# A Mamba layer and a ternary FFN on one core: the FFN's second product from float32 to three bfloat16 passes, by halves of the tokens

## The chip, the core and the metric

The kernel runs on one core of a Trainium2 chip. Five engines work from queues of their own, each strictly in order: PE (TensorE, matrix products into PSUM), DVE (VectorE), ACT (ScalarE, with function tables that are loaded when the function changes), POOL (GpSimd) and SP, which here only issues DMAs. They meet through semaphores. The metric is the device time of one run in microseconds. Inputs lie in HBM; the work sits in SBUF (128 partitions) and in the eight banks of PSUM, 512 float32 wide each.

## The reference

16 sequences of 512 tokens, 256 wide, go through a Mamba-2 block and then an FFN with ternary weights, each with layer norms and residuals. The FFN is what the change touches:

```python
def _ternary(w):
    scale = jnp.maximum(jnp.mean(jnp.abs(w)), 1e-08)
    w_t = jnp.clip(jnp.round(w / scale), -1.0, 1.0)
    return w + jax.lax.stop_gradient(w_t - w)
...
    h = jnp.einsum('bsd,fd->bsf', x, _ternary(W1)) + b1      # 256 -> 1024
    h = jax.nn.gelu(h, approximate=False)
    out = jnp.einsum('bsf,df->bsd', h, _ternary(W2)) + b2    # 1024 -> 256
...
x = x + _layernorm(mamba branch of _layernorm(x))
x = x + _layernorm(_L0_ffn_ref(_layernorm(x)))
```

The ternary weights are -1, 0 and 1, so they are exact in bfloat16. A float32 number is, to float32 accuracy, the sum of three bfloat16 pieces: its head, the head of what is left, and what is left after that. A product of float32 activations with ternary weights is then three bfloat16 products that add up in one PSUM bank.

## The kernel before

Each sequence b goes through stages, written as Python generators that yield now and then an amount of work:

- `stage_a0`, `stage_t0`: first layer norm (x1) and its transpose x1T (tile pt_a).
- `stage_a`: input projection on PE, blocks pm (lines 320 to 340, with a convolution by DVE into cv and a SiLU by ACT into xbc) and pz (line 345, SiLU into zs), the rows of dt (pq, pqt). Block 5 of pm is `stage_a5`.
- `stage_a2`: softplus of dt in small DVE steps (lines 447 to 465, tiles sp_z, sp_e, sp_a), then sums (pd), whose exponentials are `stage_b0` (dec, cum; lines 507 and 512).
- `stage_b1`: the decay matrices mt by PE (pe, line 549) and ACT's Exp. `stage_d`, `stage_e`: ct by a DMA and three POOL products (line 533).
- `stage_b2`: the scan over four chunks of 128 tokens: PE's px, pg, pst and py, DVE's xdt, bT, mt, state and y, POOL's xend, zs, state and the squares (lines 573, 574).
- `stage_c1`: output projection po, second residual x2, the FFN's norm x3, its transpose pt_f, and the three bfloat16 pieces of the transposed x3 in the tile x3p: head by ACT (739), rest by DVE (740), head of the rest by ACT (743), third piece by POOL (744).
- `stage_c2`: the FFN. For each of 8 blocks f of 128 hidden channels, `passes` makes 6 matmuls of 512 columns (3 pieces, 2 halves of the 256 inputs) into a PSUM tile ph of its own, and ACT's GELU with its bias writes hT in float32 (762). Then, for each chunk c of 128 tokens, 8 float32 matmuls (790) with hT as the loaded and `w2_sb` as the moving side give pf; DVE adds b2 (796), and the last norm and the residual follow (`finish`, by DVE 290, POOL 782 and a DMA by SP).

`interleave` merges generators: each stream has a total work and a start and end between 0 and 1, and the next step is taken from the stream that is least far along. The queues are recorded in just that order, and all four compute engines run it as recorded. A turn i of the main loop (lines 885 to 909, i from 1 to 14) has two parts. In the first, `stage_a` of sequence i+1 runs beside `stage_c1` of i-1 and `stage_e` of i. In the second, `stage_c2` of i-1 runs beside `stage_b2` of i, with `a2`, `a5`, `b0`, `b1` and `a0` of later sequences at given places. After the loop come one interleaving for the last two sequences (lines 911 to 918) and `stage_c2(15)` by itself.

PSUM: four banks (`ps_a`) serve the projections and the scan, two (`ps_tr`) transposes and small results, two (`ps_c`) po, ph and pf. Before the loop `scales` and `ternary` make the ternary weights: `w1_bf` in bfloat16, w2 in place in float32.

## Time and profile before

| | |
|---|---|
| three timed runs | 1174.28, 1177.25, 1177.72 us; median 1177.25 |
| the profiled execution | 1172.91 us |
| its span, first to last instruction | 1171.1 us |
| mean granted clock of PE | 0.98 |
| first product, L756, PE | 768 records of 128x512 bf16, 189.0 us busy |
| second product, L790, PE | 1024 records of 128x256 f32, 248.8 us busy |
| GELU, L762, ACT | 128 of 128x512, 87.8 us busy, 688 ns each, and 15 table loads of 1283 ns |

Busy time is how long an engine had an instruction running; a matmul of N columns has a record longer than the time after which the next may start, so means of PE records overlap and the steady distance between starts is read from the chain of waits. A float32 matmul shows as two records. The idle time in front of an instruction is put down to what released it. In the windows each engine's busy time is given for a stretch, with the number of instructions in brackets. The trace's clock runs from the first instruction.

### The profile page before, as it was taken

The numbers are of one execution on the slowest core, as the hardware profiler recorded it, in microseconds if no ns is written. First come the engines' busy times: TensorE is split into PE (matmuls) and PEld (weight loads), VectorE is DVE, ScalarE is ACT, GpSimd is POOL, SyncE is SP. The second block draws the span as 40 slices with busy tenths as digits, with TensorE's granted clock in tenths as the row PEclk, the third lists the DMA queues.
The fourth block names the chain that finished last, engine by engine and source line by source line (L and its number), as shares of the span: only waits on it lengthen the run. The fifth ranks groups of instructions, "written<-read, shape, count | busy, mean of one in ns | idle before, by whom it ended". The sixth has DMA issues, their size and how long they took to land.

```text
span 1171.1 us, 16958 instructions
## 1 busy us (share of the span) xinstructions
PE 1110.8 (95%) x6164; PEld 727.9 (62%) x6164; DVE 849.0 (72%) x2211; ACT 568.0 (48%) x957; POOL 593.7 (51%) x706
## 2 busy tenths in 40 slices
PE   5778999999999999999999999999999999998697
PEld 2345475665757666575766757576675757667475
DVE  5597968768686876868687686868768686875552
ACT  5625546356454635645463564546346454532321
POOL 3453546355554635555463555546355554545742
PEclk9888999999999999999999999999999999999899
DMA  5101010020201102020110202011020101002000
GB/s 194 58 1 58 18 67 27 4 76 17 75 18 65 29 4 76 17 74 19 59 35 4 73 20 75 18 58 36 4 72 20 75 18 58 19 4 72 2 10 27
DMA packets 28627, 48.57 MB, mean 41 GB/s; under 512 B 6656, under 2 KB 25728, under 8 KB 26496
## 3 DMA queue, kind: packets, MB, share of 16 engines
q1 hardware_dynamic: 26992, 47.33, 11.8%
q8 instruction: 48, 0.79, 0.3%
q10 hardware_dynamic: 1552, 0.16, 0.1%
q14 instruction: 35, 0.29, 0.1%
HBM read 38.44 MB, written 9.04 MB: 41 GB/s over the span
## 4 chain that ended last, share of the span: by engine, by line
PE 83%; DVE 6%; POOL 6%; ACT 3%; DMA 1%; issue 1%; POOLq 0%; ACTq 0%; DVEq 0%
PE pf L790 20%; PE pm L323 12%; PE ph L756 12%; PE po L710 9%; PE pz L345 8%; PE py L644 5%; PE pst L628 4%; PE py L651 3%; POOL x3p L744 3%; PE pe L549 2%; DVE cv L330 1%; POOL xend L608 1%; PE pt_a L300 1%; PE px L593 1%; PE pt_f L736 1%
## 5 line engine op out<-in xcount | busy, mean ns | idle before, releaser
L790 PE MATMUL pf<-w_sb,hT 128*128 128x256 f32 x1024 | 248.8, 383 | 0.0
L330 DVE SCALAR_TENSOR_TENSOR cv<-pm,cw_sb,cv 128x511 f32<-128x511 f32 (+2 forms) x288 | 215.3, 747 | 44.8 <-ACT cv L328 36.9
L790 PEld LDWEIGHTS pf<-w_sb,hT 128*128 128x128 f32 x1024 | 189.8, 190 | 42.3 <-issue 14.3
L756 PE MATMUL ph<-x3p,w_bf 128*128 128x512 bf16 x768 | 189.0, 381 | 4.2 <-ACT x3p L743 1.7
L661 POOL TENSOR_TENSOR zs<-y,zs 128x512 f32<-128x512 f32 x64 | 81.7, 1276 | 206.9 <-DVE y L657 206.9
L323 PE MATMUL pm<-x1T,win_sb 128*128 128x512 f32 x384 | 184.1, 602 | 0.0
L762 ACT ACTIVATE hT<-ph,b_sb 128x512 f32<-128x512 f32 x128 | 87.8, 688 | 128.2 <-PE ph L756 128.2
L756 PEld LDWEIGHTS <-w_bf 128*128 128x128 bf16 x768 | 72.9, 98 | 93.8 <-issue 29.1
L553 ACT ACTIVATE mt<-pe 128x512 f32<-128x512 f32 x128 | 73.6, 595 | 110.3 <-PE pe L549 110.3
L710 PE MATMUL po<-wo_sb,zs 128*128 128x256 f32 x512 | 124.6, 388 | 0.3 <-DVE att L716 0.3
L345 PE MATMUL pz<-x1T,win_sb 128*128 128x512 f32 x256 | 123.8, 607 | 0.3 <-DVE dt L368 0.3
L328 ACT ACTIVATE cv<-pm,cw_sb 128x512 f32<-128x512 f32 x96 | 65.7, 684 | 118.7 <-PE pm L323 117.1
L323 PEld LDWEIGHTS pm<-x1T,win_sb 128*128 128x128 f32 x384 | 70.9, 193 | 71.8 <-issue 65.7
L710 PEld LDWEIGHTS po<-wo_sb,zs 128*128 128x128 f32 x512 | 95.8, 192 | 28.3 <-issue 16.9
L533 POOL TENSOR_TENSOR ct<-ct,xbc 128x1024 f32<-128x1024 f32 x48 | 113.3, 2374 | 0.0
L657 DVE SCALAR_TENSOR_TENSOR y<-xbc,dsk,py 128x128 f32<-128x128 f32 x256 | 71.2, 340 | 37.5 <-PE py L651 20.7
L644 PE MATMUL py<-mt,xdt 128*64 128x128 f32 x1024 | 97.0, 284 | 0.0
L796 DVE TENSOR_TENSOR o<-pf,b_sb 128x256 f32<-128x256 f32 x64 | 26.8, 419 | 88.2 <-PE pf L790 88.2
L349 ACT ACTIVATE zs<-pz 128x512 f32<-128x512 f32 x64 | 37.9, 592 | 93.3 <-PE pz L345 93.3
L345 PEld LDWEIGHTS pz<-x1T,win_sb 128*128 128x128 f32 x256 | 48.0, 194 | 55.9 <-issue 47.0
L611 DVE SCALAR_TENSOR_TENSOR mt<-mt,pg 128x1024 f32<-128x1024 f32 x64 | 77.6, 1212 | 0.5
L644 PEld LDWEIGHTS py<-mt,xdt 128*64 128x64 f32 x1024 | 61.3, 140 | 26.8 <-issue 11.8
(138 smaller groups left out, 1810.1 us busy)
## 6 DMA issues: line engine op xcount, KB each, us to landing
ct<-way SPq DMA_DIRECT2D x16, 1536.0 KB
xin<-in_x SPq DMA_DIRECT2D x16, 512.0 KB, 6.7
out<-o SPq DMA_DIRECT2D x30, 256.0 KB, 2.2
w_in<-in_w SPq DMA_DIRECT2D x1, 1024.0 KB
w_sb<-in_w SPq DMA_DIRECT2D x1, 1024.0 KB
win_sb<-in_w_in SPq DMA_DIRECT2D x1, 768.0 KB, 6.2
win_sb<-in_w_in SPq DMA_DIRECT2D x1, 512.0 KB
wo_sb<-in_w_out SPq DMA_DIRECT2D x1, 512.0 KB
```

The lines of the kernel that those rows point to most:

```text
L323: nc.tensor.matmul(pm, win_sb[:, k, DI + m * P : DI + (m + 1) * P], x1T[:, k, :], start=(k == 0), stop=(k == 1),)
L330: nc.vector.scalar_tensor_tensor(cv[:, j:], pm[:, 0 : L - j], cw_sb[:, m, 3 - j : 4 - j], cv[:, j:], ALU.mult, ALU.add,)
L345: nc.tensor.matmul(pz, win_sb[:, k, j * P : (j + 1) * P], x1T[:, k, :], start=(k == 0), stop=(k == 1),)
L533: nc.gpsimd.tensor_tensor(ct[:, c - 1], ct[:, c - 1], xbc[:, 5, c * P : (c + 1) * P].unsqueeze(1).to_broadcast([P, NH, P]), ALU.mult,)
L553: nc.scalar.activation(mt[:, hs, :].rearrange("p h t -> p (h t)"), pe, AF.Exp)
L611: nc.vector.scalar_tensor_tensor(mts[c], mts[c], 1.0, cbt.unsqueeze(1).to_broadcast([P, NH, P]), ALU.min, ALU.mult)
L644: nc.tensor.matmul(py[h % 2 * HD : (h % 2 + 1) * HD, j, :], xdt[:, h * HD : (h + 1) * HD], mts[c][:, h, :], start=True, stop=(c == 0),)
L661: nc.gpsimd.tensor_tensor(zs[:, :, tok], y, zs[:, :, tok], ALU.mult)
L710: nc.tensor.matmul(po[:, 0:DM], g[:, k, c * P : (c + 1) * P], wo_sb[:, k, :], start=(k == 0), stop=(k == NJ - 1),)
L756: nc.tensor.matmul(ph, w1_bf[:, k, f * P : (f + 1) * P], x3p[:, j, k, :], start=(j == 0 and k == 0), stop=(j == 2 and k == 1),)
L762: nc.scalar.activation(hT[:, f, :], ph, AF.Gelu, bias=b1_sb[:, f : f + 1])
L790: nc.tensor.matmul(pf[:, 0:DM], hT[:, f, c * P : (c + 1) * P], w2_sb[:, f, :], start=(f == 0), stop=(f == NF - 1),)
```

## The change

Three things change.

The first product's and the GELU's results are read as bfloat16 without a cast: `upper` views a float32 tile as pairs of bfloat16 and takes every second one, the upper half of the bits. For x3 the head is the upper half of a float32 copy (`x3h`), the rest is taken against it, and the rest's upper half is the second piece; only the third is a bfloat16 tile of its own (`x3t`). ACT's casts of line 743 are gone.

The FFN runs by halves of the tokens: 256 columns in each matmul of the first product, GELU into `h` (float32). Two blocks f and f+1 share one PSUM tile from block 2 on (in the second half from block 0 on); in the instruction order as built, the matmuls of the odd block wait for the GELU of the even one. For each pair of blocks DVE subtracts (`rest`, h minus its upper half, into `hr`) and POOL subtracts (`third`, into `ht`), at the places that `later` and the second loop give. The second product is three bfloat16 passes per half, each over both chunks and 8 blocks, into two PSUM tiles that stay open through all three.

The order moves: `stage_c2`'s work is given as 20.7 instead of 24.2 (so `b0`, at half of the part, now stands between the two halves of the tokens), `b1` comes later, and after the loop `stage_c1(14)` comes first, `stage_e(15)` earlier and `stage_c2(14)` from 0.235 on. SBUF tiles change their places accordingly (rests, the staging of w1 and w2).

```diff
@@ -180,13 +181,13 @@
     wo_sb = const.tile([P, DI // P, DM], F32)
     nc.sync.dma_start(wo_sb, w_out.rearrange("(k p) n -> p k n", p=P))
 
-    w1_in = one.tile([P, NF, L], F32, tag="hT", name="w1_in")
-    w1_sb = w1_in[:, 0 : 2 * FF // L, :].rearrange("p f t -> p (f t)").rearrange(
-        "p (k n) -> p k n", k=2
-    )
+    w1_in = one.tile([P, NF, L // 2], F32, tag="h", name="w1_in")
+    w1_sb = w1_in.rearrange("p f t -> p (f t)").rearrange("p (k n) -> p k n", k=2)
     nc.sync.dma_start(w1_sb, w1.rearrange("(k p) n -> p k n", p=P))
     w1_bf = const.tile([P, 2, FF], BF16)
-    w2_sb = const.tile([P, NF, DM], F32)
+    w2_in = one.tile([P, NF, L // 2], F32, tag="hr", name="w2_in")
+    w2_sb = w2_in.rearrange("p f t -> p (f t)").rearrange("p (k n) -> p k n", k=NF)
+    w2_bf = const.tile([P, NF, DM], BF16)
     nc.sync.dma_start(w2_sb, w2.rearrange("(k p) n -> p k n", p=P))
 
     negA = const.tile([P, NH], F32)
@@ -195,10 +196,11 @@
 
 
 
-    x3p_0 = one.tile([P, 3, 2, L], BF16, tag="x3p", name="low_2")
+    low_1 = one.tile([P, NF, L // 2], BF16, tag="ht", name="low_1")
+    low_2 = one.tile([P, 2, L], F32, tag="x3h", name="low_2").bitcast(BF16)
     ternaries = {
-        1: (w1_sb, w1_in[:, 4:8, :].rearrange("p f t -> p (f t)"), w1_bf),
-        2: (w2_sb, x3p_0.rearrange("p j k t -> p (j k t)")[:, 0 : 4 * L], w2_sb),
+        1: (w1_sb, low_1.rearrange("p f t -> p (f t)"), w1_bf),
+        2: (w2_sb, low_2.rearrange("p k t -> p (k t)"), w2_bf),
     }
     halves = {}
 
@@ -235,6 +237,10 @@
             )
             yield 1.0
 
+
+    def upper(t):
+
+        return t.bitcast(BF16).rearrange("p a (t i) -> p a t i", i=2)[:, :, :, 1]
 
     class Norm:
 
@@ -682,8 +688,6 @@
         last = b == NB - 1
         if last:
             x2 = io.tile([P, NC, DM], F32, tag="xin", name=f"x2_{b}")
-            rests = io.tile([P, NC, DM], F32, tag="xin", name=f"rests_{b}")
-            rests = rests.rearrange("p c d -> p (c d)").rearrange("p (k t) -> p k t", k=2)
         else:
             x2 = one.tile([P, NC, DM], F32, tag="x2", name=f"x2_{b}")
         x3 = one.tile([P, NC, DM], F32, tag="att", name=f"x3_{b}")
@@ -727,53 +731,32 @@
             yield (0.1, 0.07, 0.01, 0.33)[c]
         norm_f.normal(x3, 0, 1, 2, 3)
         yield 0.22
-        if not last:
-            rests = one.tile([P, 2, L], F32, tag="o", name=f"rests_{b}")
-        x3p = one.tile([P, 3, 2, L], BF16, tag="x3p", name=f"x3p_{b}")
+
+
+        if b < NB - 2:
+            rests = one.tile([P, NC, DM], F32, tag="att", name=f"rests_{b}")
+        else:
+            rests = three.tile([P, NC, DM], F32, tag="x1", name=f"rests_{b}")
+        rests = rests.rearrange("p c d -> p (c d)").rearrange("p (k t) -> p k t", k=2)
+        x3h = one.tile([P, 2, L], F32, tag="x3h", name=f"x3h_{b}")
+        x3t = one.tile([P, 2, L], BF16, tag="x3t", name=f"x3t_{b}")
         for k in range(2):
             pt = ps_tr.tile([P, 512], F32, tag="tr", name=f"pt_f{b}_{k}")
             for c in range(NC):
                 nc.tensor.transpose(
                     pt[:, c * P : (c + 1) * P], x3[:, c, k * P : (k + 1) * P], ident
                 )
-            nc.scalar.copy(x3p[:, 0, k, :], pt)
-            nc.vector.tensor_sub(rests[:, k, :], pt, x3p[:, 0, k, :])
+            nc.scalar.copy(x3h[:, k, :], pt)
+            nc.vector.tensor_sub(rests[:, k, :], pt, upper(x3h)[:, k, :])
         yield 0.12
         for k in range(2):
-            nc.scalar.copy(x3p[:, 1, k, :], rests[:, k, :])
-            nc.gpsimd.tensor_sub(x3p[:, 2, k, :], rests[:, k, :], x3p[:, 1, k, :])
-        s.update(x2=x2, x3p=x3p, shift=norm_c.off)
+            nc.gpsimd.tensor_sub(x3t[:, k, :], rests[:, k, :], upper(rests)[:, k, :])
+        s.update(x2=x2, x3=(upper(x3h), upper(rests), x3t), shift=norm_c.off)
 
 
     def stage_c2(b):
         s = seqs.pop(b)
-        x2, x3p, shift = s["x2"], s["x3p"], s["shift"]
-        hT = one.tile([P, NF, L], F32, tag="hT", name=f"hT_{b}")
-
-        def passes(ph, f, lo, hi):
-            for j in range(lo, hi):
-                for k in range(2):
-                    nc.tensor.matmul(
-                        ph, w1_bf[:, k, f * P : (f + 1) * P], x3p[:, j, k, :],
-                        start=(j == 0 and k == 0), stop=(j == 2 and k == 1),
-                    )
-
-        def bent(ph, f):
-            nc.scalar.activation(hT[:, f, :], ph, AF.Gelu, bias=b1_sb[:, f : f + 1])
-
-        phs = [ps_c.tile([P, L], F32, tag="c", name=f"ph_{b}_{f}") for f in range(2)]
-        for f in range(2):
-            passes(phs[f], f, 0, 2)
-            yield 0.86
-        for f in range(2):
-            passes(phs[f], f, 2, 3)
-            bent(phs[f], f)
-            yield 0.44
-        for f in range(2, NF):
-            ph = ps_c.tile([P, L], F32, tag="c", name=f"ph_{b}_{f}")
-            passes(ph, f, 0, 3)
-            bent(ph, f)
-            yield 1.3
+        x2, x3, shift = s["x2"], s["x3"], s["shift"]
         o = one.tile([P, NC, DM], F32, tag="o", name=f"o_{b}")
         norm_o = Norm(o, f"o{b}")
 
@@ -784,27 +767,83 @@
                 out[b].rearrange("(c p) d -> p c d", p=P)[:, lo:hi], o[:, lo:hi]
             )
 
-        for c in range(NC):
-            pf = ps_c.tile([P, L], F32, tag="c", name=f"pf_{b}_{c}")
-            for f in range(NF):
-                nc.tensor.matmul(
-                    pf[:, 0:DM], hT[:, f, c * P : (c + 1) * P], w2_sb[:, f, :],
-                    start=(f == 0), stop=(f == NF - 1),
-                )
-                if f % 2 == 1 and f < NF - 1:
-                    yield 0.86
-            nc.vector.tensor_tensor(o[:, c, :], pf[:, 0:DM], b2_sb, ALU.add)
-            norm_o.stats(c)
-            if b == NB - 1:
-                norm_o.shift(c, c + 1, shift)
-                finish(c, c + 1)
-                yield 0.86
-                continue
-            if c % 2 == 1:
-                norm_o.shift(c - 1, c + 1, shift)
-            if c == 2:
-                finish(0, 2)
-            yield 0.86
+        for half in range(2):
+            T = L // 2
+            tok = slice(half * T, (half + 1) * T)
+
+            h = one.tile([P, NF, T], F32, tag="h", name=f"h_{b}_{half}")
+            hr = one.tile([P, NF, T], F32, tag="hr", name=f"hr_{b}_{half}")
+            ht = one.tile([P, NF, T], BF16, tag="ht", name=f"ht_{b}_{half}")
+            pieces = upper(h), upper(hr), ht
+
+            def passes(ph, f, lo, hi):
+                for j in range(lo, hi):
+                    for k in range(2):
+                        nc.tensor.matmul(
+                            ph, w1_bf[:, k, f * P : (f + 1) * P], x3[j][:, k, tok],
+                            start=(j == 0 and k == 0), stop=(j == 2 and k == 1),
+                        )
+
+            def bent(ph, f):
+                nc.scalar.activation(h[:, f, :], ph, AF.Gelu, bias=b1_sb[:, f : f + 1])
+
+            def rest(p):
+                fs = slice(2 * p, 2 * p + 2)
+                nc.vector.tensor_sub(hr[:, fs, :], h[:, fs, :], pieces[0][:, fs, :])
+
+            def third(p):
+                fs = slice(2 * p, 2 * p + 2)
+                nc.gpsimd.tensor_sub(ht[:, fs, :], hr[:, fs, :], pieces[1][:, fs, :])
+
+            later = {3: (rest, 0), 5: (rest, 1), 6: (third, 0), 7: (rest, 2)}
+            first = 0
+            if half == 0:
+                phs = [ps_c.tile([P, L], F32, tag="c", name=f"ph_{b}_{f}") for f in range(2)]
+                for f in range(2):
+                    passes(phs[f][:, 0:T], f, 0, 2)
+                    yield 0.43
+                for f in range(2):
+                    passes(phs[f][:, 0:T], f, 2, 3)
+                    bent(phs[f][:, 0:T], f)
+                    yield 0.22
+                first = 2
+            for f in range(first, NF):
+                if f % 2 == 0:
+                    ph = ps_c.tile([P, 2, T], F32, tag="c", name=f"ph_{b}_{half}_{f}")
+                passes(ph[:, f % 2, :], f, 0, 3)
+                bent(ph[:, f % 2, :], f)
+                yield 0.65
+                if f in later:
+                    act, p = later[f]
+                    act(p)
+                if half == 1 and f == 4:
+                    finish(0, 2)
+
+            pfs = [ps_c.tile([P, L], F32, tag="c", name=f"pf_{b}_{half}_{c}") for c in range(2)]
+            for j in range(3):
+                for c in range(2):
+                    for f in range(NF):
+                        nc.tensor.matmul(
+                            pfs[c][:, 0:DM], pieces[j][:, f, c * P : (c + 1) * P], w2_bf[:, f, :],
+                            start=(j == 0 and f == 0), stop=(j == 2 and f == NF - 1),
+                        )
+                        if f % 4 == 3:
+                            yield 0.43
+                            if j == 0:
+                                for at, act, p in (
+                                    (3, third, 1), (7, rest, 3), (11, third, 2), (15, third, 3)
+                                ):
+                                    if at == 8 * c + f:
+                                        act(p)
+                    if j == 2:
+                        at = 2 * half + c
+                        nc.vector.tensor_tensor(o[:, at, :], pfs[c][:, 0:DM], b2_sb, ALU.add)
+                        norm_o.stats(at)
+                        if b == NB - 1 and half == 1:
+                            norm_o.shift(at, at + 1, shift)
+                            finish(at, at + 1)
+            if b < NB - 1 or half == 0:
+                norm_o.shift(2 * half, 2 * half + 2, shift)
         if b < NB - 1:
             endings.append(lambda: finish(2, 4))
 
@@ -835,7 +874,7 @@
     endings = []
     E_WORK = 1.0
     A0_WORK, T0_WORK, A_WORK, A2_WORK, B1_WORK, B2_WORK = 1.0, 0.9, 18.1, 1.0, 0.5, 14.9
-    C1_WORK, C2_WORK = 1.0, 24.2
+    C1_WORK, C2_WORK = 1.0, 20.7
 
 
 
@@ -894,8 +933,8 @@
             run(stage_a1(i + 1))
             second = [
                 (stage_b0(i + 1), 0.1, 0.5, 0.51),
-                (stage_b1(i + 1, 0, 2), 2 * B1_WORK, 0.68, 0.8),
-                (stage_b1(i + 1, 2, 3), B1_WORK, 0.86, 0.9),
+                (stage_b1(i + 1, 0, 2), 2 * B1_WORK, 0.77, 0.86),
+                (stage_b1(i + 1, 2, 3), B1_WORK, 0.88, 0.92),
                 (stage_b1(i + 1, 3, 4), B1_WORK, 0.95, 0.99),
             ]
             second.append((stage_c2(i - 1), C2_WORK, 0.02, 1.0))
@@ -909,12 +948,12 @@
             interleave(*second)
         run(stage_a6(NB - 1))
         interleave(
-            (ending(), 0.1, 0.05, 0.06),
-            (stage_e(NB - 1), E_WORK, 0.0, 0.25),
-            (stage_c1(NB - 2), C1_WORK, 0.0, 0.4),
-            (stage_b2(NB - 1), B2_WORK, 0.0, 0.53),
-            (stage_c2(NB - 2), C2_WORK, 0.4, 0.98),
-            (stage_c1(NB - 1), C1_WORK, 0.54, 1.0),
+            (ending(), 0.1, 0.0, 0.01),
+            (stage_c1(NB - 2), C1_WORK, 0.0, 0.235),
+            (stage_e(NB - 1), E_WORK, 0.03, 0.16),
+            (stage_b2(NB - 1), B2_WORK, -0.02, 0.4),
+            (stage_c2(NB - 2), C2_WORK, 0.235, 0.98),
+            (stage_c1(NB - 1), C1_WORK, 0.42, 0.9),
         )
         interleave((ending(), 0.1, 0.05, 0.06), (stage_c2(NB - 1), C2_WORK, 0.0, 1.0))
 
```

## The prediction

> **What bounds the kernel now.** First the table of busy times and the costliest groups, to see the engine that never rests and what the edited lines cost. Second the windows of one turn of the main loop. Third the chain of waits and the timeline, for how a wait of PE on ACT and a clash of DVE and POOL look.
>
> ```profile
> PE 1110.8 (95%) x6164; PEld 727.9 (62%) x6164; DVE 849.0 (72%) x2211; ACT 568.0 (48%) x957; POOL 593.7 (51%) x706
> L790 PE MATMUL pf<-w_sb,hT 128*128 128x256 f32 x1024 | 248.8, 383 | 0.0
> L756 PE MATMUL ph<-x3p,w_bf 128*128 128x512 bf16 x768 | 189.0, 381 | 4.2 <-ACT x3p L743 1.7
> ```
> ```profile
> 523.00:548.00 25.00, 24.46 (x107) 14.29 (x106) 23.10 (x56) 15.36 (x27) 16.23 (x18) 1.00 0.09 32
> 548.00:591.50 43.50, 43.50 (x281) 30.55 (x280) 28.88 (x83) 19.59 (x34) 19.45 (x26) 1.00 0.13 45
> ```
> The columns are length, PE, weight loads, DVE, ACT, POOL, clock. A turn lasts 68.5 us. Its second part, where the FFN of one sequence runs beside the state work of the next, has PE busy for all of 43.5 us, with DVE at 28.9 and POOL at 19.5: PE sets the turn, and the other two stay ahead of it because their queues have gaps.
>
> ```profile
> 485.77 0.44 PE px L593 x4
> 486.54 1.29 PE ph L756 x6
> ```
> ```profile
> 1142.26 0.70 ACT hT L762
> 1142.95 0.04 issue
> 1143.00 7.93 PE ph L756 x36
> ```
> The first pair prices PE: 0.215 us for a bfloat16 matmul of 512 columns, 0.109 for one pass of 128 columns in float32. The second, from the last sequence, is the one place where PE waits for a GELU: the next block can't start until ACT is through.
>
> ```profile
> 74.49 4.46 DVE L459 SCALAR_TENSOR_TENSOR sp_a<-sp_a,sp_e 128x32 f32<-128x32 f32 x4
> 80.50 2.27 DVE L463 SCALAR_TENSOR_TENSOR dt<-sp_a,dt 128x32 f32<-128x32 f32 x1
> ```
> ```profile
> 75.88 2.34 POOL L533 TENSOR_TENSOR ct<-ct,xbc 128x1024 f32<-128x1024 f32 x1
> 78.18 0.72 POOL L573 TENSOR_TENSOR y<-y 128x256 f32<-128x256 f32 x1
> 78.98 0.45 POOL L574 TENSOR_TENSOR sq<-y 128x128 f32<-128x128 f32 x1
> 79.39 1.04 POOL L633 TENSOR_TENSOR state<-state,dec 128x512 f32<-128x512 f32 x1
> 80.39 2.34 POOL L533 TENSOR_TENSOR ct<-ct,xbc 128x1024 f32<-128x1024 f32 x1
> ```
> A DVE operation with both inputs in SBUF, 0.19 us by its median, lasts as long as the POOL operation that is running, and the two engines take turns. The new DVE subtractions have both inputs in SBUF.
>
> **What PE saves.** Per sequence the second product is 32 float32 matmuls of 256 columns, two records each, at 1.73 us for 8 records: 13.8 us. It becomes 96 bfloat16 matmuls of 256 columns. No row has that shape. Lower bound: half of 0.215, 0.1075; upper bound: the load (98 ns mean on L756) not hidden, 0.205. I take 0.109, since the transposes on L593 hide a load of 143 ns under a pass of that length: 10.46 us. The first product goes from 48 matmuls at 0.215 (10.34) to 96 at 0.109 (10.46). Saved: 3.2 us a sequence, 51 over 16.
>
> Two of three pieces are read at every second bfloat16; no row shows such a read. Bounds: nothing, or 0.215 a matmul (the float32 records, 0.215 for 256 columns) for the 64 of 96 first-product matmuls whose moving side is spread, 64 x 0.106 = +6.8 us a sequence. I take nothing, the nearest row: the float32 transposes also step by four bytes and pass 128 columns in 0.109. The Trainium skill, "SBUF — State Buffer", section "Door 1: The DMA port swizzle", has 16-byte lines that give full bandwidth while at least two accesses fall in a line, which four-byte steps meet; by it the sum has no such term either, and a rate of half would refute it here.
>
> **What it adds.** *A wait at each odd block.* Two 256-column blocks of the first product now share a PSUM tile, and in the built order the odd block's first matmul waits for the GELU of the even one. Last matmul of the even block: its record of about 0.27 us (376 ns less the 107 of the missing columns) runs 0.16 past its stream; 0.03 to ACT; GELU of 256 columns 0.47 (0.69 for 512, less 256 x 0.84 ns, the slope between the copies of 128 and 512 columns, 265 and 587 ns); 0.04 back: 0.70 us. In one turn block 3 of the first half hides it under a pst (0.86), block 5 under a py (1.02), block 3 of the second half under a pm. Uncovered: block 7, and blocks 5 and 7 of the second half, 2.1 us. Block 1 of the second half is worse: `b0`'s exponentials now fall between the halves, so ACT loads tables twice more (1.28 each). From pd on: sums, copy of cum, load, dec, cum, load, GELU: about 0.9 us of stall. Against that, PE needs 3.6 us from pd to there.
>
> *DVE and POOL.* Per sequence 8 subtractions of 512 on DVE, 0.68 each (L740), 5.4 us; 8 on POOL at 1.16 (L744), 9.3 us, minus nothing, since the two for x3 stay. ACT loses the two casts on L743 (1.23), so x3's third piece starts some 2.2 us sooner; but block 2 waits for block 0's GELU behind the table load that ended at 547.13, PE idles 1.7 us there instead of 1.1: +0.6. DVE's 28.9 and POOL's 19.5 of the second part become 34.3 and 28.8 of 40.3. That fits as a share; it does not fit as a queue. I walked the built queues from 543.16 with the rows' durations:
> - First half, second pieces. PE: from block 2's start at 547.7 six blocks of 0.65, pst 0.86, py 1.02, the wait 0.70, px and pg 0.77, 20 matmuls of pf 2.2, pst 0.86, py 1.72: it asks for blocks 4 to 7 at 559.7. DVE's queue up to rest 3, from the first y at 551.7: y 1.1, four softplus steps 0.8, rest 1 0.68, xdt 0.69, pg and bT 0.6, mt 1.2, four softplus steps 0.8, rest 2 0.68, state 0.69, rest 3 0.68. POOL's: zs up to 554.1, third 0 555.3, xend 556.3, third 1 557.5, the squares 558.7, state 559.7. With no clash DVE's state waits for that, and rest 3 ends at 561.1: a stall of 1.2. With clashes the softplus steps wait out zs and third 0, the next four get one turn per POOL operation (third 1, two squares, state), so rest 2 ends at 563.1, and rest 3, behind third 2, at 565.0: 5.1.
> - pd then waits for the softplus, queued behind rest 3: 0.1 or 1.3.
> - `b1`'s fourth exponent needs the PSUM bank that the last y frees; y stands behind rest 1 and the output's scaling: 1.2 or 1.55. The second half's second pieces then: 0 or 2.1.
> - Third pieces of the second half. When the last py ends POOL still has rs and off (1.2), the output's addition (1.27), third 0, the squares, zs behind that y, and thirds 1 to 3: by the walk 10.6 us without clashes, 12.9 with. PE asks after 6.7 or 8.5 and gets 4 matmuls in between: 3.4 or 3.9.
>
> Sum without clashes 0.6+2.1+0.9+1.2+0.1+1.2+0+3.4 = 9.5, with them 0.6+2.1+0.9+5.1+1.3+1.55+2.1+3.9 = 17.55. Less 3.2: +6.3 or +14.3 us a turn. I take two thirds of the way up, +11.7, since the clashes are shown but not each falls in step.
>
> *Clock.* After PE's idle 3.9 us up to 1090.75 and 3.2 up to 1096.87, the four pairs of py took 0.43 instead of 0.22 us, until 1106. Waits of 2 to 3.4 us recur in every turn now; I price it at 0 to +1.5 a turn, which the upper end holds. The Trainium skill, "TensorE: Matmul & The Clock Gate", "Part 1: The HAM clock gate", halves the clock after an idle window of about 3.4 us; by that rule alone only the first-half wait (3.4 us unbroken) could do it, and the shorter ones cost nothing.
>
> *Last stage.* c1 of sequence 14 goes ahead, `ct` is multiplied earlier: POOL's two ct operations at 1092.87 and 1096.41 (4.7 us) leave the chain, and some 3 us of slow clock with them: -8 (bounds 0 and -12). c2 of 14 pays 0.7 x 6 for bare odd blocks and about 1 for thirds, less 3.2: +2. c2 of 15 runs alone: 7 odd or bank waits of 0.7, less 3.2: +2. Together -4. The stage before the loop runs no FFN: 0.
>
> **Sum.** 14 turns x 11.7 = 164, less 4: 1171.1 + 160 = 1331 us of span. The profiled run took 1172.9 and the median is 1177.25, 6 us over the span: 1335 us as these runs are timed.
>
> **Rivals.**
> - *Only latencies, no clashes:* +6.3 a turn: 1171.1 + 88 - 4 + 6 = 1261. For it: POOL's share is half. Against: the rows at 74.5 to 82.8.
> - *Faster: PE's columns alone decide.* If the rests and thirds arrive before PE asks and the odd waits find cover, the saving stays: 1171.1 - 51 - 4 + 6 = 1122. It decides as soon as the waits of a turn are under 3.2 us; the 2.1 of bare odd blocks and 0.9 of table loads already use that up.
> - *Spread reads at half rate:* 6.8 a sequence on top, half of it under the waits: 1335 + 16 x 3.4 = 1389.
> - *No change that can be told:* the waits equal the saving, a turn of +0.2: about 1177.
>
> **How the numbers follow.** Forecast 0.60, latencies alone 0.25, spread reads 0.05, faster 0.07, same 0.03. The forecast's own range is 1290 to 1385 (+8.5 to +14.3 a turn, and up to 0.9 of clock). The one for 8 in 10 goes down past the latencies' 1261 to 1235 (+4.4 a turn) and up to 1390. Faster by over 0.3% 0.07, within 0.3% (about what a measurement of this kernel can tell from no change) 0.03, slower 0.90.
>
> **What would show it.** Matmuls of pf and ph in 0.11 us each where nothing waits; PE idle before ph, released by ACT's h, some 0.7 us apiece; DVE's subtractions of h averaging well over 0.68 us; PE idle before loads of hr (DVE) and ht (POOL), longest in the second half; 14 more table loads for GELU; the second part of a turn near 55 us with PE far from full, the first still near 25. I am wrong if that second part is under 43 us, or if the waits sit elsewhere.

## The result, and the profile after

The changed kernel takes 1369.49 us (median of 4 runs, 1368.08 to 1370.94) against 1177.3 us (4 runs, 1174.28 to 1177.72): ratio 1.1641, 95% interval 1.1623 to 1.1659. It is slower by 192 us. The profiled execution has a span of 1369.2 us against 1171.1, mean granted clock 0.927 against 0.980.

The page after, its busy times, its chain and the groups that answer to the second and the first product (the float32 group of 1024 and the group of 768 before):

```profile
PE 1151.0 (84%) x7444; PEld 785.0 (57%) x7444; DVE 977.1 (71%) x2338; ACT 618.4 (45%) x1081; POOL 749.4 (55%) x830
...
DVE 44%; POOL 23%; PE 21%; ACT 7%; issue 3%; DMA 1%; SPq 0%; ACTq 0%; POOLq 0%; DVEq 0%
...
L782 PE MATMUL ph<-x3h,w_bf 128*128 128x256 bf16 x512 | 102.2, 281 | 72.6 <-ACT h L788 68.0
L796 POOL TENSOR_TENSOR ht<-hr 128x512 bf16<-128x512 f32 x128 | 139.5, 1101 | 19.5 <-DVE hr L792 19.5
L826 PE MATMUL pf<-w_bf,ht 128*128 128x256 bf16 x512 | 102.7, 352 | 38.1 <-POOL ht L796 38.1
...
L826 PE MATMUL pf<-w_bf,hr 128*128 128x256 bf16 x512 | 80.7, 292 | 48.9 <-DVE hr L792 48.9
L792 DVE TENSOR_TENSOR hr<-h 128x512 f32<-128x512 f32 x128 | 110.4, 872 | 10.0 <-ACT h L788 10.0
```
The chain of the kernel before, for comparison:

```profile
PE 83%; DVE 6%; POOL 6%; ACT 3%; DMA 1%; issue 1%; POOLq 0%; ACTq 0%; DVEq 0%
```
PE, 95% busy before, is at 84%, and 67% of the chain that ended last is now DVE and POOL, where it was 12%. A group's line ends with its busy time, the mean of one in ns and, behind the second bar, the idle time of its engine in front of it. For PE that is 72.6 us before blocks of the first product, 48.9 before matmuls on hr, 38.1 before those on ht. Before the change both products together showed 4.2. DVE's new subtraction, 0.68 us alone, averages 0.87.

One turn after, by windows (columns as before: length, PE, weight loads, DVE, ACT, POOL, clock, DMA). The first two lines are the turn's two parts; the others are stretches of 3.41 us, laid so that the clock changes at their edges:

```profile
601.10:626.10 25.00, 25.00 (x103) 14.90 (x102) 21.18 (x56) 13.67 (x23) 16.78 (x20) 1.00 0.10 32
626.10:683.00 56.90, 45.98 (x365) 33.98 (x364) 38.72 (x91) 24.75 (x45) 28.74 (x31) 0.91 0.11 35
...
641.35:644.77 3.42, 2.84 (x40) 2.08 (x37) 2.82 (x6) 0.00 (x0) 3.34 (x4) 1.00 0.00 0
644.77:648.18 3.41, 0.84 (x7) 0.52 (x7) 2.90 (x7) 0.00 (x0) 2.45 (x3) 1.00 0.00 0
648.18:651.59 3.41, 3.41 (x15) 2.44 (x16) 2.25 (x9) 1.48 (x2) 1.27 (x1) 0.50 0.00 0
651.59:655.01 3.42, 3.42 (x18) 2.76 (x16) 1.03 (x3) 1.80 (x4) 0.00 (x0) 0.50 0.11 26
655.01:658.42 3.41, 2.85 (x21) 1.89 (x20) 3.21 (x7) 1.38 (x3) 0.00 (x0) 1.00 0.02 5
675.46:678.87 3.41, 0.96 (x6) 0.23 (x4) 0.00 (x0) 0.60 (x1) 3.41 (x4) 1.00 0.60 256
678.87:682.28 3.41, 3.21 (x15) 2.64 (x16) 1.03 (x3) 1.45 (x3) 0.14 (x1) 0.50 0.00 0
```
The first part is what it was, 25 us with PE full. The second went from 43.5 to 56.9 us, all of the change. PE is busy for 46.0 of it although its work fell: in three stretches of 3.41 us the granted clock is 0.50, and each such row follows one in which PE was busy for under 1 us of 3.41, or another slow one. That costs half of three stretches, 5.1 us a turn. Before, the clock of these turns was 1.00 throughout.

What PE waited for in that second part (total, times, longest):

```profile
PE ph L782 <- ACT h L788: 4.2, 5, 2.0
PE pf L826 <- DVE hr L792: 3.5, 3, 2.1
PE pf L826 <- POOL ht L796: 2.6, 3, 1.4
PE pd L483 <- DVE a L471: 0.6, 1, 0.6
```
The five waits on a GELU are 1.97 at the start and four times 0.56. The sum is 10.97 us, against one wait of 0.40 (on xend) in a turn before.

So the turn of 81.9 us (68.5 before) adds up: +10.6 of waits, +5.1 of slow clock, -3.2 of work (as predicted), which is 12.5 of 13.4. The missing 0.9 belongs to the waits as well, because a wait shows as idle only from the end of the record in front of it:

```profile
636.31 0.38 PE L782 MATMUL ph<-x3t,w_bf 128*128 128x256 bf16 x2
637.25 0.39 PE L782 MATMUL ph<-x3h,w_bf 128*128 128x256 bf16 x2 [0.56 <-ACT h L788]
```
After two matmuls at 0.11 us each the next could have started at 636.53. It started at 637.25, 0.72 us later, of which 0.56 shows. Each of the 12 waits of a turn costs 0.16 us more than its idle time, 1.9 us in all; the turn before loses 0.6 us in this way (see the pieces of x3 below). With these 1.3 us the sum is 13.8, within 0.4 of the measured 13.4.

### The profile page after: what moved, and what is told of

It is laid out like the page before. It is cut to its first block, busy times and chain, and to the rows that moved or that the text cites. A ratio compares the mean times of both kernels' runs of the same rounds, so it can differ in the third digit from the quotient of the medians.

```text
span 1369.2 us, 19821 instructions
## 1 busy us (share of the span) xinstructions
PE 1151.0 (84%) x7444; PEld 785.0 (57%) x7444; DVE 977.1 (71%) x2338; ACT 618.4 (45%) x1081; POOL 749.4 (55%) x830
## 4 chain that ended last, share of the span: by engine, by line
DVE 44%; POOL 23%; PE 21%; ACT 7%; issue 3%; DMA 1%; SPq 0%; ACTq 0%; POOLq 0%; DVEq 0%
DVE cv L336 12%; PE pf L826 7%; POOL ht L796 6%; PE ph L782 4%; POOL state L639 3%; POOL y L579 3%; DVE y L663 3%; DVE sp_a L462 2%; DVE hr L792 2%; DVE st_f L257 2%; DVE x L700 2%; PE pt_a L306 2%; ACT xbc L341 2%; DVE mt L617 2%; DVE state L642 2%
## 5 line engine op out<-in xcount | busy, mean ns | idle before, releaser
L336 DVE SCALAR_TENSOR_TENSOR cv<-pm,cw_sb,cv 128x511 f32<-128x511 f32 (+2 forms) x288 | 214.7, 745 | 23.7 <-ACT cv L334 16.4
L782 PEld LDWEIGHTS <-w_bf 128*128 128x128 bf16 x1536 | 147.9, 98 | 142.2 <-issue 119.1
L788 ACT ACTIVATE h<-ph,b_sb 128x256 f32<-128x256 f32 x256 | 119.5, 474 | 215.4 <-PE ph L782 214.1
L782 PE MATMUL ph<-x3h,w_bf 128*128 128x256 bf16 x512 | 102.2, 281 | 72.6 <-ACT h L788 68.0
L796 POOL TENSOR_TENSOR ht<-hr 128x512 bf16<-128x512 f32 x128 | 139.5, 1101 | 19.5 <-DVE hr L792 19.5
L826 PE MATMUL pf<-w_bf,ht 128*128 128x256 bf16 x512 | 102.7, 352 | 38.1 <-POOL ht L796 38.1
L826 PE MATMUL pf<-w_bf,hr 128*128 128x256 bf16 x512 | 80.7, 292 | 48.9 <-DVE hr L792 48.9
L792 DVE TENSOR_TENSOR hr<-h 128x512 f32<-128x512 f32 x128 | 110.4, 872 | 10.0 <-ACT h L788 10.0
L826 PEld LDWEIGHTS <-ht 128*128 128x128 bf16 x512 | 60.9, 126 | 74.3 <-POOL ht L796 50.1
L782 PE MATMUL ph<-rests,w_bf 128*128 128x256 bf16 x512 | 101.6, 280 | 0.0
L782 PE MATMUL ph<-x3t,w_bf 128*128 128x256 bf16 x512 | 96.4, 275 | 0.0
```

The source lines that it names most:

```text
L336: nc.vector.scalar_tensor_tensor(cv[:, j:], pm[:, 0 : L - j], cw_sb[:, m, 3 - j : 4 - j], cv[:, j:], ALU.mult, ALU.add,)
L782: nc.tensor.matmul(ph, w1_bf[:, k, f * P : (f + 1) * P], x3[j][:, k, tok], start=(j == 0 and k == 0), stop=(j == 2 and k == 1),)
L788: nc.scalar.activation(h[:, f, :], ph, AF.Gelu, bias=b1_sb[:, f : f + 1])
L792: nc.vector.tensor_sub(hr[:, fs, :], h[:, fs, :], pieces[0][:, fs, :])
L796: nc.gpsimd.tensor_sub(ht[:, fs, :], hr[:, fs, :], pieces[1][:, fs, :])
L826: nc.tensor.matmul(pfs[c][:, 0:DM], pieces[j][:, f, c * P : (c + 1) * P], w2_bf[:, f, :], start=(j == 0 and f == 0), stop=(j == 2 and f == ...
```

## The experiments

"A turn" is the mean over eight turns of the loop. The cost of the slow clock is the time at 0.5, halved.

**A PSUM tile for each block** (e1_own_bank)

```diff
-                if f % 2 == 0:
-                    ph = ps_c.tile([P, 2, T], F32, tag="c", ...)
-                passes(ph[:, f % 2, :], f, 0, 3)
-                bent(ph[:, f % 2, :], f)
+                ph = ps_c.tile([P, L], F32, tag="c", ...)
+                passes(ph[:, 0:T], f, 0, 3)
+                bent(ph[:, 0:T], f)
```


> Every 256-column block of the FFN's first product gets a PSUM tile of its own, so no block waits for the GELU of the block in the same tile; it still waits for the tile two blocks before. Theory: the bare odd waits (0.56 us, four of them in a turn, 2.2 us) go; in the first half what they gave is half given back, since PE then asks for the second pieces sooner than DVE has them. -1.2 to -2.2 us in each of 14 turns: 1339 to 1353 us. The wait of 1.97 us at the start of the second part stays (block 2 on block 0). Rival: all of it is given back, because the last subtraction on DVE and not PE sets when the second pieces are there: 1365 to 1370 us, with the waits on hr longer by what those on h lose.

Measured: 1361.07 us (1360.64 to 1361.51). The waits of one turn:

```profile
PE pf L825 <- DVE hr L792: 4.3, 3, 2.1
PE pf L825 <- POOL ht L796: 2.6, 3, 1.4
PE ph L782 <- ACT h L788: 2.0, 1, 2.0
PE ph L782 <- DVE o L839: 1.5, 1, 1.5
PE pd L483 <- DVE a L471: 0.6, 1, 0.6
```
The four odd waits are gone, and 2.3 us came back: 0.8 on hr, 1.5 on the addition that frees a bank. The turn is 81.9 us as before the edit; the 8 us that the run is faster lie behind the loop. In the loop the rival was right: the odd waits cost nothing there while DVE and POOL are behind. Removing a wait only moves PE to the next late piece.

**The third piece left out** (e2_no_third)

```diff
-            pieces = upper(h), upper(hr), ht
+            pieces = upper(h), upper(hr), upper(hr)
...
-                nc.gpsimd.tensor_sub(ht[:, fs, :], hr[:, fs, :], pieces[1][:, fs, :])
+                return
```


> POOL's third piece of h is left out, and PE reads the second piece again in its place: the matmuls are as many as before, the third piece is not in the output. Theory: in a turn the 2.6 us of waits on the third piece go, DVE's subtractions of h fall from a mean of 0.87 us to near 0.70, which takes 0.5 to 2 us from the waits on the second piece, and the granted clock has one stretch at 0.5 less (676 to 682, some 2.5 us): -5.6 to -7.1 us a turn, 1270 to 1291 us. Rival: POOL's work costs only the waits that the trace names, and the clock does not hang on them: -2.6 a turn, 1333 us.

Measured: 1227.92 us (1226.81 to 1229.12), ratio to the kernel before 1.0446 (1.0427 to 1.0464): 142 us less than the change, more than the theory's 78 to 99. The waits of one turn, and DVE's subtraction in the table of groups:

```profile
PE ph L781 <- ACT h L787: 4.2, 5, 2.0
PE pf L825 <- DVE hr L791: 1.3, 2, 0.6
```
```profile
L791 DVE TENSOR_TENSOR hr<-h 128x512 f32<-128x512 f32 x128 | 100.8, 797 | 10.6 <-ACT h L787 10.6
```
With POOL's 9 us a sequence gone, the wait on ht goes, but so do the one on pd and two thirds of that on hr (3.5 to 1.3): the subtraction falls from 872 to 797 ns, and DVE's idle time behind POOL's state from 4.5 to 3.6 us a turn. Waits fall by 5.5 us a turn and the slow clock from 5.1 to 0.6. The theory had kept one of the two slow passages; neither stayed, and what is left is one slow stretch in three turns of eight, in another place. A turn is 71.6 us.

**PE kept busy during the waits** (e3_fill)

```diff
+            extra = {(0, 1, 0, 4): 24, (1, 1, 0, 4): 9, (1, 2, 0, 2): 13,
+                     (1, 2, 0, 4): 6, (1, 2, 0, 6): 6}
...
+                        for _ in range(extra.get((half, j, c, f), 0)):
+                            nc.tensor.matmul(
+                                pfs[c][:, 0:DM], pieces[0][:, f, c * P : (c + 1) * P],
+                                w2_bf[:, f, :], start=False, stop=False,
+                            )
```


> 58 more matmuls of the second product a sequence (the first piece's, once more, 0.109 us each) are put just ahead of the matmuls that wait for second and third pieces: 24 in the first half, 34 in the second, 6.3 us of PE's time, so that PE works through most of the 6.1 us of waits. They add parts of the product twice to the output. Nothing else changes on any engine. Theory: the granted clock of 0.5 in 648 to 654 and 679 to 682 follows from the 3 to 4 us before in which PE did little; with those filled the clock stays near 1.00 and the turn loses some 5.5 us although PE has 6.3 us more to do: 1369 - 14 x 5.5 = 1292 us, 1280 to 1315. Rival: the clock falls for another reason, or the added matmuls push the waits on instead of filling them: 1369 to 1450 us.

Measured: 1332.27 us (1329.77 to 1334.13), 37 us less with 6.3 us of work more in each turn. That lies between the two expectations. The second part of one turn, to be read beside 626.10:683.00 above:

```profile
603.30:657.10 53.80, 48.97 (x425) 37.06 (x423) 38.56 (x90) 24.44 (x45) 28.63 (x31) 0.97 0.10 37
```
PE no longer waits for hr or ht at all (what is left is the 4.2 us on GELUs and 0.6 on pd), and the clock no longer falls behind those places: its cost goes from 5.1 to 1.3 us a turn. 1.3 remain because in three turns of four the clock now falls some 6 us into the second part, behind the wait of 1.97 us. So 6.3 of work, less 6.2 of waits, less 3.8 of clock: -3.7 a turn, and the turn went from 81.9 to 78.4. The rival is out: the added work about equals the waits that it fills, and the kernel still got faster by what the clock gained. The theory had taken the clock's whole cost for these two places.

**No pieces of h** (e4_no_pieces): both subtractions return at once, and

```diff
-            pieces = upper(h), upper(hr), ht
+            pieces = upper(h), upper(h), upper(h)
```


> The second and third pieces of h are left out (no subtraction on DVE or POOL); PE reads the first piece in all three passes, so its matmuls are as many as before. Theory: the waits on both pieces (6.1 us a turn), the wait of pd behind them (0.6) and the slow clock (some 5.7) go together: -12.4 us a turn, 1369 - 174 = 1195 us, 1180 to 1215. Rival: the slow clock has another cause, such as the odd waits that remain: -6.7 a turn, 1275 us.

Measured: 1206.87 us (1205.88 to 1208.75), ratio 1.0269 (1.0247 to 1.0291); a turn of 70.1 us, -11.8. Only the 4.2 us on GELUs are left, and 0.9 of slow clock behind them. The theory holds; its -12.4 was 0.6 a turn too much.

**No pieces, and a tile for each block** (e6_no_pieces_own_bank): the two edits together.

> As e4_no_pieces (the second and third pieces of h are left out, the first is read three times), and every block of the first product has a PSUM tile of its own. In e4 a turn of 69.2 or 70.9 us still has 4.2 us of waits of PE on a GELU. In e1 the four odd waits (2.2 us) went and all of it came back as a longer wait on hr and a new one of 1.54 us on the addition that frees a bank. Theory: it came back there because DVE was behind with the pieces; without them nothing takes the place of the odd waits, so -2.2 us and up to -0.6 of slow clock in each of 14 turns: 1168 to 1177 us, about the time of the kernel before. Rival: the wait for the bank is there without the pieces too: 1190 to 1207 us.

Measured: 1173.11 us (1172.29 to 1174.15), ratio 0.9973 (0.9963 to 0.9984). The odd waits go, slow clock falls to 0.2 a turn, and a wait of 1.57 on the bank is there all the same, so the rival's wait exists and the theory's time came out. This is the whole change without a single late piece, and it is worth 3 us, no more than the new order of the last stage gives by itself (4.1, next run). In the loop the 3.2 us that PE saves in a turn are spent on the start (1.97) and the bank.

**The new order of the last stage alone** (x2_before_new_end): the kernel before with the six lines of the last stage as the change has them.

> The kernel before with only the new order of the last stage. The prediction put this at -8 us (0 to -12): 1168 us, 1164 to 1176. Rival: the two ct operations only change their place in the chain and the time stays within 0.3%: 1172 to 1179 us.

Measured: 1172.46 us (1169.19 to 1173.48) beside 1176.55, ratio 0.9963 (0.995 to 0.9976): -4.1 us, half of the -8, inside its bounds (in the profiles the last stage, from the last sequence's first px on, takes 99.7 us against 105.5). PE's waits in the last stage fall from 13.2 to 9.3 us: 5.9 on xend and 1.7 on x3p go, but 1.5 more come at pt_f and 2.3 at pg, which waits for rests.

**The pieces of x3 as upper halves, alone** (x1_before_upper_x3): the kernel before with x3h, rests and x3t of the change, in tiles of 512 columns.

> The kernel before with only the pieces of x3 read as the upper halves of float32 values, so that ACT's two casts of x3 (1.23 us a sequence) go; FFN otherwise as before. Theory: spread reads cost PE nothing at 512 columns either, and ACT is off the path that sets a turn: no change in the turn, 1 to 2 us less where c2 runs alone, 1173 to 1177 us. Rival: the 64 of 96 records a turn that read spread pieces take longer than 0.215 us each: above 1180 us.

Measured: 1164.7 us (1163.37 to 1166.53), ratio 0.9902 (0.9888 to 0.9915): neither expectation; it is faster than the kernel before, with all pieces. A turn falls from 68.5 to 67.7 us. The start of the second part in the kernel before:

```profile
543.67 1.13 ACT L743 CAST x3p<-rests 128x512 bf16<-128x512 f32 x2
543.75 1.48 PE L756 MATMUL ph<-x3p,w_bf 128*128 128x512 bf16 x4
544.36 2.28 POOL L744 TENSOR_TENSOR x3p<-rests,x3p 128x512 bf16<-128x512 f32 x2 [2.31 <-ACT x3p L743]
546.60 1.04 POOL L608 TENSOR_TENSOR xend<-xdt,dec 128x512 f32<-128x512 f32 x1
547.69 1.12 PE L628 MATMUL pst<-xend,bT 128*128 128x512 f32 x2 [0.40 <-POOL xend L608]
```
POOL's third piece used to wait 2.31 us for ACT's cast and kept xend behind it; now it ends before xend is asked for, and PE's 0.40 us in front of pst are gone. Another 0.6 us go that never showed as idle time: the matmuls on the second piece came 0.46 us late behind the casts (the four from 543.75 on took 1.32 us to the next start, not 0.86), and the record in front of the wait ran on for 0.16. So ACT was on the path there, against the theory. Spread reads give some 0.3 of this back:

```profile
547.41 0.59 PE L760 MATMUL ph<-x3t,w_bf 128*128 128x512 bf16 x2
547.84 0.61 PE L760 MATMUL ph<-x3h,w_bf 128*128 128x512 bf16 x2
548.29 0.61 PE L760 MATMUL ph<-rests,w_bf 128*128 128x512 bf16 x2
548.75 0.59 PE L760 MATMUL ph<-x3t,w_bf 128*128 128x512 bf16 x2
```
Two matmuls on the dense x3t take 0.43 us to the next start, two on the spread x3h or rests 0.45 to 0.46; 32 of a turn's 48 are spread here (the 64 of 96 in the rival are those of the change).

**Two pieces over all tokens** (k8_two_pieces, k9_two_pieces_early, k10_two_pieces_all, k11_two_pieces_ahead). The kernel before, blocks of 512 columns in tiles of their own, and the following. The subtractions of blocks 6 and 7, not shown, stand in the first pass of pf, and `stage_c2`'s work is given as 17.3.

```diff
+        def rest(f):
+            nc.vector.tensor_sub(pieces[1](f), hT[:, f, :], pieces[0](f))
...
             passes(ph, f, 0, 3)
             bent(ph, f)
             yield 1.3
+            rest(f - 2)
...
+        for j, c in ((0, 0), (0, 1), (1, 0), (1, 1), (0, 2), (1, 2), (0, 3), (1, 3)):
+            for f in range(NF):
+                nc.tensor.matmul(
+                    pf[:, 0:DM], pieces[j](f)[:, c * P : (c + 1) * P], w2_bf[:, f, :],
...
```


> The kernel before, FFN over all 512 tokens with blocks of 512 columns as there, but the second product in two bfloat16 passes: the upper halves of h, and h less these, which DVE writes as bfloat16 block by block, two blocks behind the GELU. The third piece of h is left out; nothing goes to POOL. Per sequence PE has 64 matmuls at 0.109 us for 13.8 us: -6.8 us; DVE has 8 subtractions more at 0.68: 5.4 us, 57.4 of a turn then near 62. Theory: what made the changed kernel slow was that pieces were late, so with no third piece and two blocks of lead PE goes on setting the turn: 62 to 64 us a turn, 1177 - 14 x 4.5 to 6.8 = 1082 to 1114 us. Rival: DVE, 92% full and blocked by POOL at times, is late again with the pieces or with the additions that free a bank: a turn of 67 to 70 us, 1155 to 1195 us.

Measured: 1191.75 us (1185.74 to 1193.11), ratio 1.0121 (1.0094 to 1.0148): the rival. PE waits 4.4 us a turn for the last subtractions, and 2.4 go to the slow clock.

```diff
             yield 1.3
-            rest(f - 2)
+            rest(f - 1)
+            if f == NF - 1:
+                rest(f)
```


> As k8_two_pieces (second product in two bfloat16 passes, the third piece of h left out), but DVE's subtractions stand one block behind the GELU and not two, and the last two right behind block 7. In k8 the subtractions of blocks 5, 6 and 7 stood behind state (which waited for POOL, 2.79 us), three convolution steps and y: they ended at 727.9, PE asked at 722.9, idled near 5 us and ran at a clock of 0.5 for the next 6. Theory: with the new order the last subtraction ends near 720 and the wait and the slow clock go: a turn of 68.5 - 6.8 + 0.8 (xend) + 0.8 (GELU) = 63.3 us, 1177 - 14 x 5.2 = 1104 us, 1090 to 1120. Rival: DVE's queue is too full whatever the order, so that state, the convolution or the additions that free a bank are late instead: 1150 to 1190 us.

Measured: 1201.29 us (1199.53 to 1204.82), ratio 1.0229 (1.0205 to 1.0253). The timeline of DVE and then of PE in one turn:

```profile
655.97 0.68 DVE L766 TENSOR_TENSOR hrhi<-hT 128x512 bf16<-128x512 f32 x1
659.45 0.69 DVE L640 TENSOR_TENSOR state<-pst,state 128x512 f32<-128x512 f32 x1 [2.79 <-POOL state L637]
660.06 2.31 DVE L334 SCALAR_TENSOR_TENSOR cv<-pm,cw_sb,cv 128x511 f32<-128x511 f32 x3
...
663.36 1.09 DVE L661 SCALAR_TENSOR_TENSOR y<-xbc,dsk,py 128x128 f32<-128x128 f32 x4
664.36 1.28 DVE L766 TENSOR_TENSOR hrhi<-hT 128x512 bf16<-128x512 f32 x2
...
665.11 0.28 PE L812 MATMUL pf<-w_bf,hrhi 128*128 128x256 bf16 x1 [3.66 <-DVE hrhi L766]
```
The edit didn't do what it was for: the waits on hrhi are 4.7 us a turn. A `yield` hands over to the other streams, so what stands after it is queued behind their next step: state, cv, y. DVE sits idle for 2.79 us with two subtractions, whose GELUs had ended by 656.6, behind the instruction that waits.

> As k9_two_pieces_early (third piece of h left out), with the pieces of x3 read as the upper halves (x1: -0.8 us a turn, -11.9 us in all) and the new order of the last stage (x2: -4.1 us). Theory: they add up, since the one takes ACT's casts from the start of the second part and the other touches only the end: 12 to 16 us below k9. Rival: the start of the second part is held by something else once PE has less to do there, so that only the end's 4 us remain: 2 to 6 us below k9.

Measured: 1184.9 us (1176.67 to 1187.28, 8 runs), ratio 1.0073 (1.0051 to 1.0095): 16.4 below k9, as the sum of x1 and x2 has it (11.9 and 4.1). The waits on hrhi are still 4.6 us a turn.

```diff
             bent(ph, f)
+            if f == NF - 1:
+                rest(f - 1)
+                rest(f)
             yield 1.3
-            rest(f - 1)
-            if f == NF - 1:
-                rest(f)
+            if f < NF - 1:
+                rest(f - 1)
```


> As k10_two_pieces_all (third piece of h left out), but the subtractions of blocks 6 and 7 are issued with block 7, before the other streams' next step. In k9 they had been meant to end near 720 but came after that step: they still stood behind state, three convolution steps and y (k9: DVE idle 2.79 us in front of state, PE idle 3.66 in front of hrhi), so k9 and k10 did not test the order. Built order now: subtractions 5, 6 and 7 back to back ahead of state. Theory: they end about 1.5 us after block 7's GELU, before PE asks; the 4.6 us of waits and some 2.3 us of slow clock a turn go: 1185 - 14 x 6 = 1101 us, 1085 to 1120. Rival: DVE then makes state, y or the bank-freeing additions late by as much: 1150 to 1190 us.

Measured: 1137.53 us (1135.44 to 1138.13), ratio 0.9653 (0.9637 to 0.9669), the fastest here; the third piece of h is not in it. The timeline of one turn, DVE and then the waits of PE:

```profile
557.58 1.89 DVE L766 TENSOR_TENSOR hrhi<-hT 128x512 bf16<-128x512 f32 x3
561.62 0.69 DVE L640 TENSOR_TENSOR state<-pst,state 128x512 f32<-128x512 f32 x1 [2.15 <-POOL state L637]
...
564.60 0.39 PE L553 MATMUL pe<-rhs_e,lhs_e 128*128 128x512 bf16 x1 [1.24 <-DVE cv L334]
566.77 0.44 PE L648 MATMUL py<-mt,xdt 128*64 128x128 f32 x4 [1.78 <-DVE y L661]
```
Two subtractions moved ahead of one waiting instruction are worth 47 us. No matmul of a turn waits for hrhi. PE now waits for DVE's cv and y, some 2.9 us a turn, so half of the theory's 6 us fell due again a little later: the turn is 66.4 us (69.3 in k10), with 0.9 of slow clock.

**The changed kernel with its pieces earlier** (a11_pieces_ahead)

```diff
-            later = {3: (rest, 0), 5: (rest, 1), 6: (third, 0), 7: (rest, 2)}
+            later = {2: (0,), 4: (1,), 6: (2,), 7: (3,)}
...
+                for p in later.get(f, ()):
+                    rest(p)
+                    third(p)
                 yield 0.65
-                if f in later:
-                    act, p = later[f]
-                    act(p)
...
-                            if j == 0:
-                                for at, act, p in (
...
```


> The changed kernel with all three pieces, nothing left out or added: rest p is issued with block 2p+2 (the last with block 7), third p right behind it, both before the other streams' next step. Same instructions, only earlier in DVE's and POOL's queues. Theory: what PE waited for was the place in the queues, so the 3.5 us of waits on hr, most of the 2.6 on ht and the 0.6 of pd shrink to 1 to 3 us in all and the slow clock with them: -7 to -11 us a turn, 1369 - 14 x 7 to 11 = 1215 to 1271 us. Rival: the thirds' 9.3 us on POOL and the turns that DVE and POOL take make the pieces late wherever they stand, or xdt, y and state, now behind them, come late: -3 us a turn or less, 1327 to 1390 us.

Measured: 1280.49 us (1278.18 to 1282.08), ratio to the kernel before 1.0871 (1.0854 to 1.0888): 89 us less than the change with the same instructions. One turn's waits:

```profile
PE ph L782 <- ACT h L788: 4.2, 5, 2.0
PE pd L483 <- DVE a L471: 2.5, 1, 2.5
PE pe L555 <- DVE y L663: 1.5, 1, 1.5
```
All 6.2 us on hr and ht are gone and the slow clock costs 2.1 instead of 5.1, but 3.3 us came in where the softplus (ahead of pd) and y now stand behind the pieces. The turn is 75.5 us, -6.4, a little under the theory's -7 to -11. So the place in the queues is about half of the loss (89 of 192 us). Of the other half, by the runs above, some 74 us go when the subtractions go (e4's 1207 us against 1280) and some 34 with the odd waits (e6's 1173 against e4's 1207). With the added work, 9 us on POOL and 5 on DVE, something was late in both placings; whether a third would do better was not tried.

## Why the prediction was nearly right

The sign, the mechanism and the range (1235 to 1390) held; the point was 34 us low. (Its last step should read 1337, not 1335: 1331 us and 6.) That it came so near is partly luck, since two terms were wrong in opposite directions. By its own steps, in us a turn (the measured waits are idle time):

| Step | Predicted | Measured |
|---|---|---|
| work of PE | -3.2 | -3.2, and +0.9 that came with the waits but does not show as idle time |
| start of the second part | +0.6 (1.7 for 1.1) | +1.6 (1.97 for 0.40) |
| odd waits: three bare, and block 1 of the second half | 2.1 + 0.9 | 1.7 + 0.56 |
| hr, first half | 1.2 to 5.1 | 2.6 |
| pd | 0.1 to 1.3 | 0.56 |
| bank of pe | 1.2 to 1.55 | 0 |
| hr, second half | 0 to 2.1 | 0.9 |
| ht, second half | 3.4 to 3.9 | 2.6 |
| slow clock | 0 to 1.5, none in the point | 5.1 |
| turn | +11.7 (+6.3 to +14.3) | +13.4 |

- *The clock was mis-sized.* The step took 0 to +1.5 as the price of "waits of 2 to 3.4 us". In a turn after, no wait is longer than 2.05, and the price is 5.1; e3 shows that it belongs to the waits on hr and ht.
- *The clashes were oversized.* "Two thirds of the way up" gave 14.9 us of waits; 10.6 came as idle time, 11.5 with the 0.9, nearer to the no-clash bound of 9.5. The clashes exist (subtractions up to 1.5 us, 872 ns in the mean, 797 without the thirds) but most of the walk's stalls did not fall in step; e2 gives what the thirds cost with all that follows, 10 of the 13.4 us a turn. The two errors nearly cancelled: -3.4 and +5.1.
- *Spread reads* cost nothing on h, where the weights are read, as taken: 0.109 us a matmul. On the moving side two matmuls on x3h or rests take 0.23 us, two on the dense x3t 0.22, some 0.35 us a turn where the prediction had nothing. The half rate would have put ph at 0.215 a matmul and is refuted. The rule of the Trainium skill that the prediction weighed ("SBUF — State Buffer", "Door 1: The DMA port swizzle") has such reads at full bandwidth; the runs have them some 5% slower, and the measurement decides.
- *Odd waits* came as priced: 0.56 of idle time and 0.16 under the record in front are 0.72, where the prediction had 0.70.
- *Table loads.* 14 more came, as said, but hid: the wait there was a plain odd wait.
- *The start* was 0.5 us too small, on the side of after: PE loses 2.1 us there (1.97 and 0.16), not 1.7. Before, it loses 1.0, near the prediction's 1.1, of which 0.40 shows as idle time; the rest is part of the 0.9 above.
- *Bank of pe:* "y stands behind rest 1" was right in the queue, but PE arrives there later than the walk said, as it is held up before that; a11 removes the earlier waits, and 1.5 us appear there.
- *Last stage:* -4 predicted; from the last sequence's first px on, it takes 116.5 us against 105.5: +11. The new order is worth -4.1 (x2; -5.8 in the profiles of the last stage), not -8. c2 of sequence 15 takes 35.6 against 31.3, +4.3 where +2 was said; the other 11 or 12, where c2 of 14 and c1 of 15 run side by side, were not taken apart. The 14 turns took 183 us more where 164 were said. Another 4 us of the span lie ahead of them, where the runs here differ by up to 5 us whatever the kernel.
- *Signs.* The longest single wait is in the first half (2.05 on hr), not in the second.
- *Rivals.* "Latencies only" (+6.3) is refuted by e2 and e3, but its waits were closer to what came than the forecast's. "PE's columns alone" is what e6 shows, at no gain rather than -55 us, since start and bank wait take it.

## What to carry to other kernels

When work is moved from the engine that sets the pace to engines that had room, ask not whether their busy time fits but when each result is asked for, and what stands ahead of it in an in-order queue: moving two subtractions ahead of one waiting instruction was worth 47 us, moving all pieces earlier 89. Short waits of the matrix engine that cluster cost more than their length, because the clock falls behind them; price them by how much of each few microseconds it is busy, not by the longest gap. Try the parts of a bundle alone: the small one (x3's pieces, ratio 0.990) was a gain that the whole buried.

## What the runs showed of the hardware

- The granted clock changes on a fixed grid of 3.413 us, in every run, and is 0.50 or 1.00 over a whole stretch. What decides is how much of the stretch before PE was busy. Stretches at full clock, over eleven turns of each of the 14 profiled kernels (from sequence 2's first px to sequence 13's):

```
PE busy share    next at 0.50   next at 1.00
under 0.30             75              0
0.30 to 0.40           10              0
0.40 to 0.45           30             21
0.45 to 0.50            2             21
0.50 to 0.60            0             49
over 0.60               0           2884
```
So the edge is near 0.43 of a stretch, some 1.9 us of idle time in any number of pieces. The Trainium skill, "TensorE: Matmul & The Clock Gate", "Part 1: The HAM clock gate (the "warmup" mystery)", has a free-running window of 3413 ns and a fall to half behind an idle one. The window agrees. As a rule on idle gaps over about 3.4 us, as the same part puts it under "HAM oscillation", it does not: with 2.05 us as the longest wait of a turn the clock fell twice in each turn, and the measurement decides.
- A slow stretch can be followed by another although PE is full in it (648.18 and 651.59 above, 3.41 of 3.41 busy). The runs do not show why.
- The turn of the changed kernel and of e1 is 81.9 us, which is 24 such stretches, although e1 has no odd waits. Whether the grid holds a turn at such a length was not tried.
- Reading every second bfloat16 costs a matmul some 5% as moving side (0.45 to 0.46 us for two of 512 columns against 0.43, in x1), and nothing that shows as weights (274 ns a record on hT, 278 on the dense hrhi, in k11).
